# Fetching a second token column by row DMAs from ScalarE, with output rows and layer blocks a step later, in a recommender forward pass

## The chip, the cores and the metric

The kernel runs on one core of one Trainium2 chip. The metric is device time in microseconds (us). A median of three runs without a profiler is the time that counts; one more execution was recorded by the hardware profiler, and everything that is read line by line comes from it.

## The reference

For each of 16384 rows of the batch:

```python
tok = word_emb[token_idx].mean(axis=1)            # 32 tokens, table 50000 x 300, f32
e1, e2, e3 = emb_mh1[mh1_idx].mean(axis=1), ...   # 20 lookups each, tables 1000/5000/10000 x 64
o1, o2, o3, o4 = emb_oh1[oh1_idx], ...            # one lookup each, tables 100/50/20/1000 x 64
emb = concatenate([tok, e1, e2, e3, o1, o2, o3, o4])          # 748 columns
wide = sum over the same small lookups of their wide_* weights  # one number per row
h = relu(emb @ W1 + b1); h = relu(h @ W2 + b2); h = relu(h @ W3 + b3)   # 1024, 512, 256
out = sigmoid(h @ Wd + bd + wide)
```

The token means need 16384 x 32 rows of 1200 bytes from device memory. The small tables are held on the chip and looked up by multiplication with counts.

## The kernel before

**Tiles and steps.** The batch is cut into 128 tiles of 128 rows. A tile has 11 steps (`STEPS`), and 27 more steps (`WAKE`) close the run: 1435 steps in one Python loop that writes out the order of the instructions of every engine by hand. A step has, in order: the next one-hots, the counts, part of the small sums, columns and rows of fetched tokens, tokens, part of the layers, the evictions that are due.

**Tokens.** `tokens()` walks 16 pairs of tokens per tile. For each token GpSimd issues an indirect DMA (line 303) that gathers 128 rows, one per partition, into a pair buffer `tok_rows` (6 buffers). Three pairs later `add_up` adds the two on VectorE (lines 279, 281, 286) into a sum in PSUM; the last addition of a tile writes its features `g`.

**Fetched tokens.** For tiles from 4 on whose number is not a multiple of three (83 tiles) the last token, number 31, isn't gathered by GpSimd. `load_column` (line 320) loads that column of indices into one partition, on SP's queue; `column_offsets` (lines 329, 330) turns them into byte offsets on VectorE. Then `fetch` loads 32 offsets at a time into SP's registers (line 338) and issues 128 DMAs of one row each on SP (line 347), spread over `FETCH_STEPS` = 16.5 steps. It starts 25 or 19.5 steps before the tile's sum is due (`FETCH_AHEAD`). The tile of rows is `fetched`, with two buffers.

**Small lookups.** VectorE compares keys with an iota to make one-hots `hot` (line 402), ScalarE scales their upper half (line 409), TensorE multiplies pairs of one-hots into counts `pc` (line 420), ScalarE evicts these to `cnt` (line 423). The one-hots are made a step before they are counted. A tile later TensorE multiplies the counts with the tables (`terms`, line 455) and VectorE reduces the sums into `g` (line 445).

**Layers.** A finished tile's features are transposed (line 496) and evicted to `x` with a scale (line 500). Tiles are put together in blocks of three (32 blocks), near the end of two (12) and one (8). A block's layers are a generator: `layer` issues f32 matmuls into one of two PSUM buffers `ph` (line 573) and leaves the eviction to ScalarE (line 584) pending until the last matmul of the next group. The driving loop asks the generator for as much work as the step's share. After the third layer `mlp` multiplies with the column `Wd` into `po` (line 605). `finish`, which is queued in `rows_out` and flushed a step later, adds `wide` on VectorE (line 612), takes the sigmoid on ScalarE (line 613) and leaves the store to SP (line 617) two steps on. A block's layers start in the same step in which its last transposes have been issued, after a `flush` of their evictions.

The part of the loop that drives the fetches:

```python
for at, t_f in fetches:
    if step == int(at) - COLUMN_AHEAD:
        load_column(t_f)
    if step == int(at) - COLUMN_LAG:
        column_offsets(t_f)
    if step == int(at):
        fetching.append((at, Paced(fetch(t_f))))
for at, rows in list(fetching):
    rows.to(P * (step + 1 - at) / FETCH_STEPS)
```

Of the kernel before, what the change touches and what calls it, by code (L numbers as in the profile page):

```python
# [19 lines left out]
P = 128  # L20
N_TOK, TOK_D = 32, 300
# [9 lines left out]
FETCH_AHEAD = {1: 25.0, 2: 19.5}  # L31
COLUMN_AHEAD = 4
COLUMN_LAG = 1
LOADS = 32
ROW_BYTES = 4 * TOK_D
WAKE = 27
# [41 lines left out]
def kernel(  # L78
# [209 lines left out]
    def tokens():  # L288

        under_way = []  # L290
        for n in range(n_all):
            if n < n_all - TOK_LAG:
                t, q = divmod(n, n_groups)
                it = token_indices[t // NSUB][:, t % NSUB, :].bitcast(U32)
                tok_rows = tokp.tile([P, TOK_GROUP * TOK_D], F32, name="tok_rows")
                rows = []
                for r in range(TOK_GROUP):
                    j = q * TOK_GROUP + r
                    if j == N_TOK - 1 and t in fetched:
# [3 lines left out]
                    nc.gpsimd.indirect_dma_start(  # L303
                        out=rows[-1],
                        out_offset=None,
                        in_=word,
                        in_offset=bass.IndirectOffsetOnAxis(ap=it[:, j : j + 1], axis=0),
                    )
# [5 lines left out]
    fetched, columns = {}, {}  # L314
    word_bytes = word.bitcast(U8).rearrange("n d -> (n d)").unsqueeze(0)

    def load_column(t):
# [6 lines left out]
    def column_offsets(t):  # L324


        column = columns[t]
        low = ROW_BYTES & -ROW_BYTES
        nc.vector.tensor_single_scalar(column, column, ROW_BYTES // low, op=ALU.mult)
        nc.vector.tensor_single_scalar(column, column, low.bit_length() - 1, op=ALU.logical_shift_left)  # L330

    def fetch(t):


        rows = fp.tile([P, TOK_D], F32, name="fetched").bitcast(U8)
        column = columns.pop(t)
        for p0 in range(0, P, LOADS):
            _, values = nc.values_load_multi_w_load_instructions(
                column[:, p0 : p0 + LOADS],
                engines=[mybir.EngineType.SP],  # L340
                min_val=0,
                max_val=(word.shape[0] - 1) * ROW_BYTES,
                skip_runtime_bounds_check_because="the indices are rows of the table",
            )
            for i, value in enumerate(values):
                p = p0 + i
                nc.sync.dma_start(out=rows[p : p + 1, :], in_=word_bytes[:, bass.ds(value, ROW_BYTES)])  # L347
                if p == P - 1:
                    fetched[t] = rows.bitcast(F32)
                yield 1  # L350

    def load_indices(blk):
# [186 lines left out]
    def flush_rows():  # L539
        while rows_out:  # L540
            rows_out.pop(0)()
# [8 lines left out]
    def flush_outputs():  # L550
        while pending:
            pending.pop(0)()
# [5 lines left out]
    def layer(dst, weights, bias, srcs, n_out, part=None):  # L558


        n = N_of(srcs[0])
        for m in range(n_out):
            begun = part is not None and m < len(part)
            ph = part[m] if begun else ps_h.tile([P, N], F32, name="ph", tag="ph")
            for k, src in enumerate(srcs):
                if begun and k < N_EARLY:
                    continue
                if k == len(srcs) - 1:
                    flush_outputs()
# [12 lines left out]

            def evict(m=m, ph=ph):
                nc.scalar.activation(dst[:, m, 0:n], ph[:, 0:n], AF.Relu, bias=bias[:, m : m + 1])  # L584

            pending.append(evict)
            yield 1

    def mlp(block, part=None):


        n = block.n
        flush_rows()
        h1 = hp.tile([P, M1, N], F32, name="h1", tag="odd")
        yield from layer(h1, w1_sb, b1_sb, [block.chunk(k) for k in range(NK)], M1, part)
        h2 = hp.tile([P, M2, N], F32, name="h2", tag="even")
        yield from layer(h2, w2_sb, b2_sb, [h1[:, k, 0:n] for k in range(M1)], M2)
        flush_outputs()
        h3 = hp.tile([P, M3, N], F32, name="h3", tag="odd")
        yield from layer(h3, w3_sb, b3_sb, [h2[:, k, 0:n] for k in range(M2)], M3)  # L600
        po = ps_h.tile([1, N], F32, name="po", tag="ph")
        for k in range(M3):
            if k == M3 - 1:
                flush_outputs()
            nc.tensor.matmul(  # L605
                po[:, 0:n], wd_sb[:, k : k + 1], h3[:, k, 0:n], start=(k == 0), stop=(k == M3 - 1)
            )
            yield 1

        def finish():  # L610
            y = block.wide()
            nc.vector.tensor_add(y, po[:, 0:n].rearrange("o (a b) -> o a b", b=P), y)
            nc.scalar.activation(y, y, AF.Sigmoid, bias=bd_sb)
# [74 lines left out]
    fetches = [(summed_at(t) - FETCH_AHEAD[t % 3], t) for t in range(FETCH_FROM, tiles) if t % 3]  # L688
    fetching = []

    def speed(step):
# [27 lines left out]
    for step in range(n_steps):  # L719
# [30 lines left out]
        if waiting and step >= waiting[0][0]:  # L750
            _, k, ks = waiting[0]
            if k in summed or ks[0] < N_EARLY and k == tiles - 1:
# [9 lines left out]
        for at, t_f in fetches:  # L762
            if step == int(at) - COLUMN_AHEAD:
                load_column(t_f)
            if step == int(at) - COLUMN_LAG:
                column_offsets(t_f)
            if step == int(at):
                fetching.append((at, Paced(fetch(t_f))))
        for at, rows in list(fetching):
            rows.to(P * (step + 1 - at) / FETCH_STEPS)  # L770
            if step + 1 - at >= FETCH_STEPS:
                rows.finish()
                fetching.remove((at, rows))
# [78 lines left out]
```

## Time and profile before

| what | value |
|---|---|
| median of 3 runs | 5056.46 us (5055.42 to 5058.48) |
| the profiled execution | 7254.38 us, its span 7252.4 us |
| granted TensorE clock in the profile | 0.879 |
| busy in the profile: TensorE, VectorE, ScalarE, GpSimd | 5570.4, 3767.8, 2743.5, 3800.6 us |
| gathers by GpSimd (line 303) | 4013, mean 947 ns |
| row DMAs by SP (line 347) | 10624 of 1.2 KB |
| DMA engines, share of the span: software queue, hardware queue | 31.5%, 2.0% |

How to read it: the profiled execution took over 2000 us more than the runs. Busy times and the lengths of single instructions are those of that one execution; shares of the span are shares of its longer time. In the groups of instructions a line gives the source line, the engine, the operation, the tile written and read, the count, busy us and mean ns, and after the bar the idle time of the engine just before these instructions with what ended most of it. "issue" means that the engine waited for nothing the profile shows. In the timeline the columns are start and length in us, and in brackets the idle time before.

### The profile page before, as it was taken

To read this page: it belongs to the slowest core of one execution; us is meant where nothing else is said; L and a number is where in the kernel's file an instruction comes from. 1 tells how busy PE (TensorE), PEld (TensorE's weight loads), DVE (VectorE), ACT (ScalarE), POOL (GpSimd) and SP (SyncE) were. 2 spreads that over 40 slices of the span, in tenths; PEclk is the share of its full clock that TensorE was granted. 3 is DMA by queue.
4 is the path that set the end of the run, shared out by engine and by line. 5 is a ranking of instruction groups with operands and counts; after the bars stand their busy time and mean duration, and the time that the engine had idled before them with its cause. 6 is when DMAs were issued, how large, how long until landed. Compare 5 with 4: busy or idle time off the path is not lost. (4 is left out here: it accounts for less than half of the span.)

```text
span 7252.4 us, 117093 instructions
## 1 busy us (share of the span) xinstructions
PE 5570.4 (77%) x36252; PEld 4062.8 (56%) x36252; DVE 3767.8 (52%) x6830; ACT 2743.5 (38%) x3658; POOL 3800.6 (52%) x4020
## 2 busy tenths in 40 slices
PE   5687777777777777777777777777777777777777
PEld 3455555555555555555555555555555666666676
DVE  4555555555555555555555555555555555555542
ACT  4343333333333333333333333333333433333331
POOL 5555555555555555555555555555555555555543
PEclk8788988888898988898888888889888988888988
DMA  5333333333333333333333333333333333333332
GB/s 154 89 91 89 90 92 90 88 91 90 88 91 89 89 91 88 89 91 90 88 87 92 90 89 89 87 88 92 91 90 87 91 89 86 85 89 90 87 82 63
DMA packets 282526, 653.63 MB, mean 90 GB/s; under 512 B 140443, under 2 KB 151707, under 8 KB 281895
## 3 DMA queue, kind: packets, MB, share of 16 engines
q0 software_dynamic: 192624, 616.65, 31.5%
q1 hardware_dynamic: 89271, 29.49, 2.0%
q8 instruction: 283, 4.64, 0.3%
q14 instruction: 348, 2.85, 0.1%
HBM read 645.64 MB, written 0.07 MB: 89 GB/s over the span
## 5 line engine op out<-in xcount | busy, mean ns | idle before, releaser
L303 POOL DMA_INDIRECT tok_rows<-in_word_emb_dram,it x4013 | 3799.7, 947 | 3405.5 <-DVE own L286 2018.9
L455 PE MATMUL pg<-terms,cnt 128*128 128x195 bf16 x17664 | 2028.9, 264 | 753.1 <-issue 571.2
L455 PEld LDWEIGHTS <-cnt 128*128 128x128 fp8e3 x17664 | 1656.0, 104 | 985.5 <-issue 934.1
L402 DVE TENSOR_TENSOR hot<-own,sc 128x1656 bf16<-128x1656 bf16 (+1 forms) x1408 | 1393.7, 990 | 1440.3 <-remote 1036.4
L423 ACT ACTIVATE cnt<-pc 128x828 uint16<-128x828 f32 (+1 forms) x1408 | 1187.3, 843 | 2083.2 <-remote 1458.4
L573 PE MATMUL ph<-x,w_sb 128*128 128x384 f32 (+5 forms) x4932 | 1674.6, 479 | 212.8 <-issue 83.9
L409 ACT ACTIVATE hot<-hot 64x768 bf16<-64x768 bf16 (+1 forms) x1408 | 1155.3, 820 | 1729.5 <-DVE hot L402 1470.2
L573 PE MATMUL ph<-h,w_sb 128*128 128x384 f32 (+2 forms) x4160 | 1357.2, 467 | 106.1 <-issue 52.5
L573 PEld LDWEIGHTS ph<-x,w_sb 128*128 128x128 f32 (+1 forms) x4932 | 922.0, 211 | 597.6 <-issue 204.2
L420 PEld LDWEIGHTS <-hot 128*128 128x128 bf16 x8192 | 639.8, 104 | 894.2 <-issue 470.8
L420 PE MATMUL pc<-hot 128*128 128x138 bf16 x8192 | 817.7, 236 | 393.9 <-ACT hot L409 211.6
L573 PEld LDWEIGHTS ph<-h,w_sb 128*128 128x128 f32 x4160 | 767.1, 208 | 413.3 <-issue 121.5
L445 DVE TENSOR_REDUCE g<-pg 128x130 f32<-128x390 f32 (+1 forms) x512 | 260.8, 509 | 1352.4 <-remote 566.9
L281 DVE TENSOR_TENSOR own<-own,tok_rows 128x300 f32<-128x300 f32 x1920 | 916.9, 478 | 67.8 <-DMA tok_rows<-in_word_emb_dram,it 5.9
L286 DVE TENSOR_TENSOR own<-own,tok_rows 128x300 f32<-128x300 f32 x1792 | 856.8, 478 | 65.6 <-DMA tok_rows<-in_word_emb_dram,it 3.9
L584 ACT ACTIVATE h<-ph,b_sb 128x384 f32<-128x384 f32 (+2 forms) x723 | 378.9, 525 | 646.5 <-remote 402.1
L500 DVE TENSOR_TENSOR x<-pc,scale 128x768 f32<-128x768 f32 x127 | 121.0, 953 | 218.3 <-PE pc L496 111.4
L389 DVE COPY sc<-pc 128x512 bf16<-128x512 bf16 x64 | 44.2, 690 | 259.6 <-remote 139.8
L605 PE MATMUL po<-h,wd_sb 128*1 128x384 f32 (+2 forms) x208 | 84.3, 494 | 121.6 <-issue 59.9
L496 PE MATMUL pc<-ident,g 128*128 128x128 f32 x762 | 125.5, 307 | 45.7 <-ACT cnt L423 31.0
L496 PEld LDWEIGHTS pc<-ident,g 128*128 128x128 f32 x762 | 97.1, 160 | 59.6 <-ACT cnt L423 39.8
L605 PEld LDWEIGHTS po<-h,wd_sb 128*1 128x1 f32 x208 | 9.0, 81 | 175.6 <-ACT h L584 82.2
(56 smaller groups left out, 497.3 us busy)
## 6 DMA issues: line engine op xcount, KB each, us to landing
fetched<-in_word_emb_dram SPq DMA_DIRECT2D x10624, 1.2 KB
tok_rows<-in_word_emb_dram,it POOLq DMA_INDIRECT x4013
ix<-in_idx_dram SPq DMA_DIRECT2D x64, 64.0 KB
w_sb<-in_W_dram SPq DMA_DIRECT2D x6, 512.0 KB
raw<-in_mh_dram SPq DMA_DIRECT2D x4, 682.5 KB
it<-in_idx_dram SPq DMA_DIRECT2D x64, 32.0 KB
w_sb<-in_W_dram SPq DMA_DIRECT2D x1, 2048.0 KB
column<-in_idx_dram SPq DMA_DIRECT2D x83, 0.5 KB
```

What stands on the lines that cost most here:

```text
L281: nc.vector.tensor_add(tok_sum, tok_sum, a)
L286: nc.vector.tensor_add(to, tok_sum, b)
L303: nc.gpsimd.indirect_dma_start(out=rows[-1], out_offset=None, in_=word, in_offset=bass.IndirectOffsetOnAxis(ap=it[:, j : j + 1], axis=0),)
L402: nc.vector.tensor_tensor(hot[:, 0 : 2 * rows, :].rearrange("p i (n d) -> p i n d", d=2), iota.rearrange("p (n d) -> p n d", d=2).unsqueez ...
L409: nc.scalar.activation(upper, upper, AF.Copy, scale=UPPER)
L420: nc.tensor.matmul(pc[:, k // n, at : at + n_h], hot[:, 2 * k, 0:P], hot[:, 2 * k + 1, :], start=True, stop=True)
L423: nc.scalar.activation(cnt[:, :, b : b + rows].rearrange("l h (g k) -> l h g k", g=2), pc[:, :, 0 : n * n_h].rearrange("l g (k h) -> l h g ...
L445: nc.vector.tensor_reduce(field_columns(features(t), pair), pg[:, 0:n, :].rearrange("p f (c d) -> p f d c", c=3), AX.X, ALU.add,)
L455: nc.tensor.matmul(pg[:, j, :], by_slice[:, h, :], terms[:, h, :], start=(h == h0), stop=(h == h1 - 1))
L496: nc.tensor.transpose(pt[:, j // n, j % n, :], g[:, c : c + P], ident)
L573: nc.tensor.matmul(to, weights[: src.shape[0], k, m * P : (m + 1) * P], src, start=(k == 0), stop=(k == len(srcs) - 1),)
L584: nc.scalar.activation(dst[:, m, 0:n], ph[:, 0:n], AF.Relu, bias=bias[:, m : m + 1])
```

## The change

Three parts.

1. Thirty tiles, 8, 12, ..., 124, have token 30 fetched too, in the same manner but on ScalarE's queue: `load_column` and `column_offsets` as before for its column, then 8 offsets at a time into ScalarE's registers, and 128 row DMAs issued by ScalarE over 38 steps, begun 42 steps before the sum is due. The rows have one buffer of their own. The column of offsets lies in bytes that two constants (`minus_count`, `zeros`), used only while the tables are converted at the start, leave free.
2. The output row. The matmuls with `Wd` move from `mlp` into `finish`; `wide` is added by a one-row matmul into the same PSUM group, so the addition on VectorE goes, and the sigmoid reads PSUM. `finish` is flushed at the latest after the first group of the next block's first layer. The tiles `h1`, `h2`, `h3` are allocated when first written.
3. A block's layers start at the earliest in the step after the one in which its last transposes were issued, and no `flush` stands before them.

```diff
+SCALAR_FROM, SCALAR_EVERY = 8, 4
+SCALAR_STEPS = 38.0
+SCALAR_AHEAD = 42.0
+SCALAR_LOADS = 8
...
+    fa = ctx.enter_context(tc.tile_pool(name="fetched_scalar", bufs=1))
...
-    minus_count = const.tile([P, P], BF16, name="minus_count")
+    early_use = const.tile([P, P // 2 + ROW], I32, name="early_use")
+    minus_count = early_use[:, 0 : P // 2].bitcast(BF16)
...
-    zeros = const.tile([P, ROW], F32, name="zeros")
+    zeros = early_use[:, P // 2 : P // 2 + ROW].bitcast(F32)
...
-                    if j == N_TOK - 1 and t in fetched:
-                        rows.append(fetched.pop(t))
+                    if (t, j) in fetched:
+                        rows.append(fetched.pop((t, j)))
                         continue
...
-        columns[t] = fp.tile([1, P], I32, name="column")
+        columns[t, j] = early_use[0:1, 0:P] if j < N_TOK - 1 else fp.tile([1, P], I32, name="column")
         nc.sync.dma_start(
-            out=columns[t], in_=idx[t * P : (t + 1) * P, N_TOK - 1 : N_TOK].rearrange("n o -> o n")
+            out=columns[t, j], in_=idx[t * P : (t + 1) * P, j : j + 1].rearrange("n o -> o n")
         )
...
-    def fetch(t):
+    def fetch(t, j):
-        rows = fp.tile([P, TOK_D], F32, name="fetched").bitcast(U8)
-        column = columns.pop(t)
-        for p0 in range(0, P, LOADS):
+        by_scalar = j < N_TOK - 1
+        rows = (fa if by_scalar else fp).tile([P, TOK_D], F32, name="fetched").bitcast(U8)
+        column = columns.pop((t, j))
+        queue, engine = (
+            (nc.scalar, mybir.EngineType.Activation) if by_scalar else (nc.sync, mybir.EngineType.SP)
+        )
+        loads = SCALAR_LOADS if by_scalar else LOADS
+        for p0 in range(0, P, loads):
             _, values = nc.values_load_multi_w_load_instructions(
-                column[:, p0 : p0 + LOADS],
-                engines=[mybir.EngineType.SP],
+                column[:, p0 : p0 + loads],
+                engines=[engine],
...
-                nc.sync.dma_start(out=rows[p : p + 1, :], in_=word_bytes[:, bass.ds(value, ROW_BYTES)])
+                queue.dma_start(out=rows[p : p + 1, :], in_=word_bytes[:, bass.ds(value, ROW_BYTES)])
...
         for m in range(n_out):
+            if rows_out:
+                if m:
+                    flush_rows()
+                else:
+                    flush_outputs()
...
-        flush_rows()
-        h1 = hp.tile([P, M1, N], F32, name="h1", tag="odd")
+        h1, h2, h3 = h("h1", M1, "odd"), h("h2", M2, "even"), h("h3", M3, "odd")
...
-        po = ps_h.tile([1, N], F32, name="po", tag="ph")
-        for k in range(M3):
-            if k == M3 - 1:
-                flush_outputs()
-            nc.tensor.matmul(
-                po[:, 0:n], wd_sb[:, k : k + 1], h3[:, k, 0:n], start=(k == 0), stop=(k == M3 - 1)
-            )
-            yield 1
 
         def finish():
+            po = ps_h.tile([1, N], F32, name="po", tag="ph")
+            po = po[:, 0:n].rearrange("o (a b) -> o a b", b=P)
             y = block.wide()
-            nc.vector.tensor_add(y, po[:, 0:n].rearrange("o (a b) -> o a b", b=P), y)
-            nc.scalar.activation(y, y, AF.Sigmoid, bias=bd_sb)
+            nc.tensor.matmul(po, ident[0:1, 0:1], y, start=True, stop=False)
+            for k in range(M3):
+                nc.tensor.matmul(
+                    po,
+                    wd_sb[:, k : k + 1],
+                    h3()[:, k, 0:n].rearrange("p (a b) -> p a b", b=P),
+                    start=False,
+                    stop=(k == M3 - 1),
+                )
+            nc.scalar.activation(y, po, AF.Sigmoid, bias=bd_sb)
...
-    mlp_work = NK * M1 + M1 * M2 + M2 * M3 + M3
+    mlp_work = NK * M1 + M1 * M2 + M2 * M3
...
+    fetches += [
+        (summed_at(t) - SCALAR_AHEAD, SCALAR_STEPS, t, N_TOK - 2)
+        for t in range(SCALAR_FROM, tiles, SCALAR_EVERY)
+    ]
...
                 if not block.missing:
                     complete.append(block)
-        if complete and layers is None:
-            flush(step)
-            block = complete.pop(0)
-            layers, target = start(block), 0
+                    completed = step
+        if complete and layers is None and step > completed:
+            layers, target = start(complete.pop(0)), 0
...
     Paced(mlp(block, part)).finish()
+    flush_outputs()
     flush_rows()
```

More of the change, by code (lines that the diff above doesn't have):

```diff
@@ L315, with load_column, column_offsets @@
     word_bytes = word.bitcast(U8).rearrange("n d -> (n d)").unsqueeze(0)
-    def load_column(t):
-        columns[t] = fp.tile([1, P], I32, name="column")
+    def load_column(t, j):
+        columns[t, j] = early_use[0:1, 0:P] if j < N_TOK - 1 else fp.tile([1, P], I32, name="column")
         nc.sync.dma_start(
-            out=columns[t], in_=idx[t * P : (t + 1) * P, N_TOK - 1 : N_TOK].rearrange("n o -> o n")
+            out=columns[t, j], in_=idx[t * P : (t + 1) * P, j : j + 1].rearrange("n o -> o n")
         )
-    def column_offsets(t):
-        column = columns[t]
+    def column_offsets(t, j):
+        column = columns[t, j]
         low = ROW_BYTES & -ROW_BYTES
@@ L346, in fetch @@
                 p = p0 + i
-                nc.sync.dma_start(out=rows[p : p + 1, :], in_=word_bytes[:, bass.ds(value, ROW_BYTES)])
+                queue.dma_start(out=rows[p : p + 1, :], in_=word_bytes[:, bass.ds(value, ROW_BYTES)])
                 if p == P - 1:
-                    fetched[t] = rows.bitcast(F32)
+                    fetched[t, j] = rows.bitcast(F32)
                 yield 1
@@ L583, in evict @@
             def evict(m=m, ph=ph):
-                nc.scalar.activation(dst[:, m, 0:n], ph[:, 0:n], AF.Relu, bias=bias[:, m : m + 1])
+                nc.scalar.activation(dst()[:, m, 0:n], ph[:, 0:n], AF.Relu, bias=bias[:, m : m + 1])
             pending.append(evict)
@@ L592, in mlp, with h, get @@
         n = block.n
-        flush_rows()
-        h1 = hp.tile([P, M1, N], F32, name="h1", tag="odd")
+        hidden = {}
+        def h(name, m, tag):
+            def get():
+                if name not in hidden:
+                    hidden[name] = hp.tile([P, m, N], F32, name=name, tag=tag)
+                return hidden[name]
+            return get
+        h1, h2, h3 = h("h1", M1, "odd"), h("h2", M2, "even"), h("h3", M3, "odd")
         yield from layer(h1, w1_sb, b1_sb, [block.chunk(k) for k in range(NK)], M1, part)
-        h2 = hp.tile([P, M2, N], F32, name="h2", tag="even")
-        yield from layer(h2, w2_sb, b2_sb, [h1[:, k, 0:n] for k in range(M1)], M2)
+        yield from layer(h2, w2_sb, b2_sb, [h1()[:, k, 0:n] for k in range(M1)], M2)
         flush_outputs()
-        h3 = hp.tile([P, M3, N], F32, name="h3", tag="odd")
-        yield from layer(h3, w3_sb, b3_sb, [h2[:, k, 0:n] for k in range(M2)], M3)
-        po = ps_h.tile([1, N], F32, name="po", tag="ph")
-        for k in range(M3):
-            if k == M3 - 1:
-                flush_outputs()
-            nc.tensor.matmul(
-                po[:, 0:n], wd_sb[:, k : k + 1], h3[:, k, 0:n], start=(k == 0), stop=(k == M3 - 1)
-            )
-            yield 1
+        yield from layer(h3, w3_sb, b3_sb, [h2()[:, k, 0:n] for k in range(M2)], M3)
         def finish():
+            po = ps_h.tile([1, N], F32, name="po", tag="ph")
+            po = po[:, 0:n].rearrange("o (a b) -> o a b", b=P)
             y = block.wide()
-            nc.vector.tensor_add(y, po[:, 0:n].rearrange("o (a b) -> o a b", b=P), y)
-            nc.scalar.activation(y, y, AF.Sigmoid, bias=bd_sb)
+            nc.tensor.matmul(po, ident[0:1, 0:1], y, start=True, stop=False)
[8 more added lines that the diff above has]
+            nc.scalar.activation(y, po, AF.Sigmoid, bias=bd_sb)
             b0 = block.first * P
@@ L686, in summed_at @@
         return n / FRONT_PACE if n < front else FRONT_STEPS + (n - front) / pace
-    fetches = [(summed_at(t) - FETCH_AHEAD[t % 3], t) for t in range(FETCH_FROM, tiles) if t % 3]
+    fetches = [
+        (summed_at(t) - FETCH_AHEAD[t % 3], FETCH_STEPS, t, N_TOK - 1)
+        for t in range(FETCH_FROM, tiles)
+        if t % 3
+    ]
+    fetches += [
+        (summed_at(t) - SCALAR_AHEAD, SCALAR_STEPS, t, N_TOK - 2)
+        for t in range(SCALAR_FROM, tiles, SCALAR_EVERY)
+    ]
     fetching = []
@@ L757 @@
                     complete.append(block)
-        if complete and layers is None:
-            flush(step)
-            block = complete.pop(0)
-            layers, target = start(block), 0
-        for at, t_f in fetches:
+                    completed = step
+        if complete and layers is None and step > completed:
+            layers, target = start(complete.pop(0)), 0
+        for at, n, *of in fetches:
             if step == int(at) - COLUMN_AHEAD:
-                load_column(t_f)
+                load_column(*of)
             if step == int(at) - COLUMN_LAG:
-                column_offsets(t_f)
+                column_offsets(*of)
             if step == int(at):
[L768 to L771, printed above, removed]
+                fetching.append((at, n, Paced(fetch(*of))))
+        for entry in list(fetching):
+            at, n, rows = entry
+            rows.to(P * (step + 1 - at) / n)
+            if step + 1 - at >= n:
                 rows.finish()
-                fetching.remove((at, rows))
+                fetching.remove(entry)
         toks.to(tokens_by(step + 1))
```

## The prediction

> **What bounds the kernel now.** I read the page's engine totals first, then the groups of instructions, then GpSimd's timeline, and last the waits.
>
> ```profile
> PE 5570.4 (77%) x36252; PEld 4062.8 (56%) x36252; DVE 3767.8 (52%) x6830; ACT 2743.5 (38%) x3658; POOL 3800.6 (52%) x4020
> ...
> L303 POOL DMA_INDIRECT tok_rows<-in_word_emb_dram,it x4013 | 3799.7, 947 | 3405.5 <-DVE own L286 2018.9
> ```
>
> By shares TensorE (PE) looks like the limit at 77%, and GpSimd (POOL) idles 3405 us. But this execution took 7254.38 us and the median of the runs is 5056.46 us, so the profile shows 2198 us that the runs don't have. The shares can't be read as they stand; I look for what the extra time is and which engine's work fills 5056 us.
>
> GpSimd's timeline from 3013 us, and SP's beside it:
>
> ```profile
> 3013.99 0.95 POOL L303 DMA_INDIRECT tok_rows<-in_word_emb_dram,it  x1 [0.30 <-issue]
> 3015.24 0.95 POOL L303 DMA_INDIRECT tok_rows<-in_word_emb_dram,it  x1 [0.30 <-issue]
> 3016.49 0.95 POOL L303 DMA_INDIRECT tok_rows<-in_word_emb_dram,it  x1 [0.30 <-issue]
> 3017.74 0.94 POOL L303 DMA_INDIRECT tok_rows<-in_word_emb_dram,it  x1 [0.30 <-issue]
> 3018.99 0.95 POOL L303 DMA_INDIRECT tok_rows<-in_word_emb_dram,it  x1 [0.31 <-issue]
> ```
> ```profile
> 3010.14 5.75 SPq L347 DMA_DIRECT2D fetched<-in_word_emb_dram  x19
> ```
>
> A gather starts 1.25 us after the one before: 0.947 busy and 0.30 in which it waits for nothing shown. This period is the commonest of all (median of the 4012 start-to-start times 1.250 us). Now 4012 × 1.2505 = 5017 us, against 5056.5 in the runs; what is left, 39.5 us, must hold the head and the tail. The first gather starts at 2.96 us, the last one here:
>
> ```profile
> 7205.74 0.95 POOL L303 DMA_INDIRECT tok_rows<-in_word_emb_dram,it  x1 [0.30 <-DVE own L286]
> ...
> 7249.77 0.40 ACT L613 ACTIVATE x<-x,bd_sb 1x128 f32<-1x128 f32 x1 [0.78 <-DVE x L612]
> ```
>
> So head and tail were 3 and 46.6 us, the tail with a halt of TensorE of some 8 us. They already fill the remainder. In an undisturbed run the gathers run back to back: **GpSimd is the bound**, its idle time an effect of this profile. The extra 2198 us fits stretches in which SP's row issues and TensorE's matmuls come 0.70 us apart for 3 to 7 us at a time (3006.6 to 3010.2, 3015.9 to 3021.3) while the gathers keep their 1.25 us; outside them SP issues a row each 0.3 us (5.75 us for 19 above; the commonest step is 0.323). Summed over SP's and TensorE's records I estimate such stretches at 2650 to 2900 us, enough for the difference. Then GpSimd waits for rows to be added (its waits, longest first):
>
> ```profile
> POOL tok_rows L303 <- DVE own L286: 2018.9, 602, 12.7
> ```
>
> **How near the others are.** In undisturbed stretches a 384-wide f32 matmul record takes 0.325 us (4 in 1.46 us less the drain), a 195-wide bf16 one 0.086, a 138-wide one 0.060. Times their counts (5632 records of 384, 2112 of 256 at 0.218, 1408 of 128 at 0.112: 2448 us; L455 1519; L420 492; the rest some 250) TensorE needs about 4710 us: 93% of 5056, the second bound. VectorE needs 3768 us plus gaps, some 80%. A row on SP costs 0.323 us (29 ns move, 228 ns issue, gaps) and each 32 offsets a register load of 2.04 us, so a fetched token takes SP 128 × 0.323 + 4 × 2.2 = 50.2 us, and 83 of them 4167 us (82%). ScalarE (ACT) is busy 2743 us (54%), 1.91 us per step over 1435 steps of 3.52 us.
>
> **What the Trainium skill says.** "Advanced Engine Details and Errata" (Sequencer Loop, Engine Queue Depths): an engine instruction is pushed into a queue, 8 deep on ScalarE, where it waits for its semaphores, while the sequencer goes on to control instructions. That would let DMA issues run beside activations; ScalarE issues none in this trace. "Perfetto Trace Analysis" (DMA Instruction — HWDGE) has one descriptor generator behind a lock, shared by its sequencers; the trace shows SP alone, 228 ns each. "DMA: Bandwidth & Descriptors" (Issuing engines are not separate DMA queues) says that a second issuing engine saves only issue time; that is what is sought here, and the DMA engines are 31.5% + 2% busy. Its section Latency and other measured facts gives a register load a floor of some 600 ns; 2.04 us for 32 registers is the nearest row.
>
> **The change, part by part.**
>
> 1. *Gathers removed.* Tiles 8, 12, ..., 124, 30 of them, lose the gather of token 30. 30 × 1.2505 = **37.5 us off the binding engine**. GpSimd's queue has nothing else. The gathers that follow start one period sooner; the 6 pair buffers (12 gathers, 15 us) let GpSimd run that far ahead of VectorE's additions.
>
> 2. *Rows on ScalarE.* 30 × 128 = 3840 row issues, each with its move, and 30 × 16 loads of 8 offsets. At SP's 0.323 us a row and 0.6 us a load (2.04/4 = 0.51 from below, 2.04 from above) a token is 41.3 + 9.6 = 50.9 us, 1528 us in all, spread over 38 steps: 1.34 us on each of 1140 steps. Behind a burst (3.4 rows and 0.4 of a load) stand the layer evictions and the next step's scaling of the one-hots; TensorE waits for both. Even one after the other, 1.91 + 1.34 = 3.25 us is below the new step of 3.50. The one-hots are scaled a step before they are counted and a layer has a second PSUM buffer, so I count it at 0, with 0.25 us per step as the cover. Bounds: -0 (no reason for a gain) and, if it all stands on the path, the second rival's price.
>
> 3. *Rows' landing.* Issue ends 4 steps, 14 us, before the sum; VectorE's wait for the fetched rows was 0.6 us in all with SP's 3-step margin. 0. The single buffer is free 3 steps before the next fetch.
>
> 4. *Columns.* SP gets 30 more loads of 0.41 us and some gap, about 20 us (4167 to 4190, hidden in 5020); VectorE 60 more scalings, 30 × (239 + 226) ns = 14 us.
>
> 5. *Output row.* VectorE loses 52 additions (L612: 17.1 + 4.9 + 2.2 = 24 us). TensorE gains 52 matmuls of one row, two records each: 64 × 0.325 + 24 × 0.218 + 16 × 0.112 = 28 us (42 by the mean of L605's row). It loses the wait for the last eviction ahead of L605, 142 us here in 57 waits, most in halts; I take 1 us × 52. TensorE ends at 4690 to 4740 of 5020. On the path: 0. The sigmoid then reads PSUM, and SP's store waits for it as before, with rows queued behind it on SP.
>
> 6. *Layers a step later.* TensorE no longer meets a block whose x is just being evicted (69 us by L500 here); hidden, 0. At the end a step's layer work (about 2 us) may slip behind the last gather, and the last row loses a hop to VectorE (0.5 us). I add 1 us; bounds -1 to +3.
>
> **Sum.** On the median: head 3 + 3982 × 1.2505 + tail 36.5 = 5019, and 1 = **5020 us**, -0.7%. The profiled execution (7254) is not bound by gathers and gets about 8200 more records; it will rather be longer, and I sum against the runs only. An effect under 0.2% (10 us) can't be told from none here.
>
> **Rivals.**
>
> *TensorE takes over at once (0.07).* If the gather in an undisturbed run takes less than 1.25 us, TensorE with 4710 us and its unseen dependences bounds the run, 28 us more and about 50 us of waits less. For: 93% is near. Against: 4012 periods fill the time to within 10 us. Time: 5056 - 22 = 5034 to 5066. That the change takes no gathers away is excluded by the code: `fetched` is looked up by (tile, token).
>
> *ScalarE's in-order issue (0.16), slower.* Place: the rows between the eviction of counts (L423) and the next scaling (L409). If the sequencer handles a row only when the activations ahead are done, each of 1140 steps costs 1.91 + 1.34 and the two gaps of clean steps (0.23 and 0.25), 3.73 us instead of 3.50: +262 us, 5282. It decides from 0.25 us exposed per step; 0.33 gives 5020 + 1140 × 0.08 = 5111. For: ScalarE stands on the chain one-hot, scaling, count. Against: ScalarE waited 1470 us for VectorE's one-hots, time in which rows can go out.
>
> *SP starved by the shared generator (0.07), slower.* Three tiles give SP 2 × 50.2 + 4 us of 117.3 now. From 50 ns more per row it is late, and VectorE stops at L286. At 70 ns: 20 ns × 256 × 41 = +210 us. A lock held 0.2 us for 3.4 rows in 3.5 us meets SP a fifth of the time: 20 ns on average, below the point.
>
> **Numbers.** The first case has 0.70: 5003 to 5050, the low end if the 10 us by which head, tail and gathers overfill the runs come off the tail and some 7 us of small stalls go too, the high end if 30 us of ScalarE's bursts show. With 0.07 for TensorE's case and some 0.08 of the slower cases' 0.23 the range runs to 5111, rounded to 5110, and leaves about 0.15 out. Faster by over 0.2% (below 5046): 0.68 of the first case and 0.02 of TensorE's, 0.70. Within 0.2%: the rest of these two and 0.01 of the slower ones, 0.08. Slower: 0.22.
>
> **What would show it.** L303 with 3983 gathers, still 1.25 us apart where not held; new row issues on ScalarE's queue near 228 ns; L409 and L423 no later after VectorE and TensorE than now; SP's row at 323 ns still; no wait of VectorE for fetched rows; L612 gone. The forecast is wrong if rows on ScalarE take much over 0.33 us, or activations wait behind them, or SP's rows slow by over 50 ns.

## The result, and the profile after

The changed kernel takes 5947.38 us (median of five runs, 5942.94 to 5951.95); the kernel before beside it 5056.46 us (5055.42 to 5058.54). The ratio is 1.1759 (95% interval 1.1746 to 1.1773): 891 us slower, where 5020 us was forecast. The profiled execution of the changed kernel has a span of 5940.9 us, so its profile can be read as its runs. The profiled execution of before (7254 us), and one group of experiments below in which before took 7368 us without a profiler, belong to a rarer kind of execution in which the whole program takes over 40% longer; no conclusion below rests on them.

The page of the changed kernel: engine totals, then the groups of the gathers, of the column offsets and of the last addition of a tile with rows from SP. After the bar stands the idle time of the engine just before these instructions, and what ended most of it.

```profile
PE 4988.0 (84%) x36356; PEld 3850.3 (65%) x36356; DVE 3756.7 (63%) x6838; ACT 2735.6 (46%) x3658; POOL 3770.0 (63%) x3990
...
L309 POOL DMA_INDIRECT tok_rows<-in_word_emb_dram,it x3983 | 3769.1, 946 | 2143.2 <-DVE own L292 921.9
...
L335 DVE TENSOR_SCALAR column<-column 1x128 int32<-1x128 int32 x83 | 17.9, 215 | 995.1 <-DMA column<-in_idx_dram 987.7
...
L292 DVE TENSOR_TENSOR g<-own,fetched 128x300 f32<-128x300 f32 x83 | 39.1, 471 | 179.9 <-DMA fetched<-in_word_emb_dram 178.4
```

The gathers are as short as ever (946 ns) and there are 30 fewer, but GpSimd now waits 922 us for additions on VectorE, and VectorE has a new stop of 988 us: at line 335, where it waits for a column of indices to arrive. In the profile of before the same two groups of VectorE hardly wait (lines 329 and 286 there), and in experiment 1 below, an execution of the usual length, they wait as little (0.0 and 0.3 us):

```profile
L286 DVE TENSOR_TENSOR g<-own,fetched 128x300 f32<-128x300 f32 x83 | 39.0, 470 | 3.4 <-DMA fetched<-in_word_emb_dram 0.6
...
L329 DVE TENSOR_SCALAR column<-column 1x128 int32<-1x128 int32 x83 | 19.8, 239 | 0.3 <-issue 0.3
```

Columns are loaded by SP. The new row DMAs on ScalarE look harmless in themselves. So the question is why SP is late.

SP's own waits in the changed kernel (engine, line, what it waited for: us in total, times, longest):

```profile
SPq L358 <- DMA fetched<-in_word_emb_dram: 1280.6, 1424, 14.6
```

SP's row DMAs (line 358) wait 1281 us for *earlier row DMAs*. A smaller wait of this kind was in the profile of before, and the prediction did not look at it:

```profile
SPq L347 <- DMA fetched<-in_word_emb_dram: 157.8, 351, 1.6
```

That execution took 7254 us; in experiment 1, of the usual length and with SP's rows alone, such waits add up to 37 us by the single records.

The single records give the reason. Each DMA of SP and of ScalarE signals its completion on one of eight semaphores, numbered 101 to 108, and the two engines share the eight. Of the row DMAs of the changed kernel none starts sooner than 1.21 us after the one before it on its semaphore, and the ones that had to wait start some 1.9 us after it. The trace also has the signals of landing: of the 2014 rows of both engines that start over 0.15 us after the instruction before them, three quarters start 15 to 20 ns after the last such signal on their own semaphore. So a DMA goes out when the previous one on its semaphore has landed. I added up the time SP stands before a row by whose DMA was last on that semaphore: **1177 us in 1172 waits behind a row of ScalarE**, 197 us behind its own.

The timeline shows one such hold. The columns are start and length in us, engine, line, operation; in brackets the idle time before.

```profile
3005.48 10.99 SPq L358 DMA_DIRECT2D fetched<-in_word_emb_dram  x16
...
3007.52 0.21 DVE L335 TENSOR_SCALAR early_use<-early_use 1x128 int32<-1x128 int32 x1 [3.55 <-DMA early_use<-in_idx_dram]
...
3011.33 0.84 ACT L420 ACTIVATE hot<-hot 64x768 bf16<-64x768 bf16 x1 [4.18 <-DVE hot L413]
...
3012.48 1.39 ACTq L358 DMA_DIRECT2D fetched<-in_word_emb_dram  x4
```

SP needs 11 us for 16 rows here. By its single records it issues a row at 3010.70, wants to issue the next at about 3010.96 on semaphore 101, and can only at 3014.46. The DMA before it on 101 is the first row of ScalarE, issued at 3012.48, whose last signal of landing comes at 3014.44; that row stands behind a load of offsets, which starts at 3011.34, with the activation of line 420 (3011.33) that had waited 4.18 us for VectorE's one-hots; and VectorE had itself stood 3.55 us waiting for a column from SP. The waits close a circle: SP, ScalarE, VectorE, SP.

What that does to SP as a whole, from its records (first row of one token to first row of the next, mean over 82 intervals):

| kernel | a token, first to last row | pause to the next token | period |
|---|---|---|---|
| parts 2 and 3 of the change alone | 51.1 us | 7.8 us | 58.9 us |
| the changed kernel | 66.8 us | 2.8 us | 69.9 us |

The first column holds all that SP does between the two rows: loads of offsets, of columns and of indices. A load of 32 offsets takes 2.1 us, so a pause of 2.8 us is no pause: SP's queue hardly rests. 82 x (69.9 - 58.5) = 935 us, with 58.5 the period of the version with separate semaphores below; that version's span is 917 us shorter. So the lengthening of SP's period is as large as the whole loss; that SP is the cause and not carried along by a kernel that is slow for another reason, experiments 3 to 5 have to show.

### The profile page after: what moved, and what is told of

Its sections match the earlier page's. It is cut to its first block, busy times and chain, and to the rows that moved or that the text cites. A ratio compares the mean times of both kernels' runs of the same rounds, so it can differ in the third digit from the quotient of the medians.

```text
span 5940.9 us, 125681 instructions
## 1 busy us (share of the span) xinstructions
PE 4988.0 (84%) x36356; PEld 3850.3 (65%) x36356; DVE 3756.7 (63%) x6838; ACT 2735.6 (46%) x3658; POOL 3770.0 (63%) x3990
## 4 chain that ended last, share of the span: by engine, by line
PE 57%; SPq 13%; DMA 11%; DVE 9%; issue 6%; ACT 2%; POOL 1%; ACTq 1%; DVEq 0%; POOLq 0%
PE ph L589 29%; PE pg L466 19%; SPq L358 10%; PE pc L431 6%; DMA fetched<-in_word_emb_dram 5%; DVE hot L413 3%; DMA column<-in_idx_dram 3%; SPq L349 3%; DVE own L287 2%; DVE own L292 2%; DMA tok_rows<-in_word_emb_dram,it 2%; ACT hot L420 1%; POOL tok_rows L309 1%; PE pc L507 1%; PE po L631 1%
## 5 line engine op out<-in xcount | busy, mean ns | idle before, releaser
L466 PE MATMUL pg<-terms,cnt 128*128 128x195 bf16 x17664 | 1804.2, 256 | 212.4 <-DVE g L456 212.4
L466 PEld LDWEIGHTS <-cnt 128*128 128x128 fp8e3 x17664 | 1592.5, 101 | 217.3 <-issue 176.2
L589 PE MATMUL ph<-x,w_sb 128*128 128x384 f32 (+5 forms) x4932 | 1517.8, 447 | 50.1 <-ACT h L600 35.7
L431 PEld LDWEIGHTS <-hot 128*128 128x128 bf16 x8192 | 610.2, 100 | 1092.1 <-ACT hot L420 718.0
L589 PE MATMUL ph<-h,w_sb 128*128 128x384 f32 (+2 forms) x4160 | 1263.0, 444 | 34.9 <-ACT h L600 34.9
L431 PE MATMUL pc<-hot 128*128 128x138 bf16 x8192 | 759.1, 230 | 613.3 <-ACT hot L420 575.5
L589 PEld LDWEIGHTS ph<-x,w_sb 128*128 128x128 f32 (+1 forms) x4932 | 856.7, 196 | 356.1 <-ACT h L600 41.2
L589 PEld LDWEIGHTS ph<-h,w_sb 128*128 128x128 f32 x4160 | 722.0, 196 | 300.1 <-ACT h L600 42.5
L292 DVE TENSOR_TENSOR g<-own,fetched 128x300 f32<-128x300 f32 x83 | 39.1, 471 | 179.9 <-DMA fetched<-in_word_emb_dram 178.4
```

Source lines behind the costliest of these rows:

```text
L292: nc.vector.tensor_add(to, tok_sum, b)
L431: nc.tensor.matmul(pc[:, k // n, at : at + n_h], hot[:, 2 * k, 0:P], hot[:, 2 * k + 1, :], start=True, stop=True)
L466: nc.tensor.matmul(pg[:, j, :], by_slice[:, h, :], terms[:, h, :], start=(h == h0), stop=(h == h1 - 1))
L589: nc.tensor.matmul(to, weights[: src.shape[0], k, m * P : (m + 1) * P], src, start=(k == 0), stop=(k == len(srcs) - 1),)
```

## The experiments

In all of them "bound by gathers" means head, tail and 1.2505 us a gather: n x 1.2505 + 39.5 us for n gathers, which is within 1 us the sum of the prediction.

**1. Parts 2 and 3 of the change alone** (output rows and blocks a step later, no token for ScalarE).

```diff
-        for t in range(SCALAR_FROM, tiles, SCALAR_EVERY)
+        for t in range(SCALAR_FROM, 0, SCALAR_EVERY)
```

> The changed kernel without ScalarE's rows: only the output row by TensorE and the layers a step later are left, gathers stay 4013. Theory (SP and ScalarE share eight completion semaphores for their row DMAs, and a row is issued only when the last row on its semaphore has landed, so SP waits for rows that ScalarE has not yet issued): no rows on ScalarE, so 5056 within 10 us. Rival A (ScalarE's rows delay its own activations): the same, 5056. Rival B (the new order of layers and output rows costs the time): about 5900.

5055.11 us against 5057.27, ratio 0.9995 (0.9986 to 1.0004). These parts cost and bring nothing. Its profiled span is 5054.4 us, and its gathers start 1.2511 us apart on average over the whole run: the reading that gathers run back to back in undisturbed runs was right.

**2. Part 1 alone** (ScalarE's rows, with the layers and output rows of before).

```diff
...
-        h1, h2, h3 = h("h1", M1, "odd"), h("h2", M2, "even"), h("h3", M3, "odd")
+        flush_rows()
+        h1 = hp.tile([P, M1, N], F32, name="h1", tag="odd")
...
-        if complete and layers is None and step > completed:
-            layers, target = start(complete.pop(0)), 0
+        if complete and layers is None:
+            flush(step)
+            block = complete.pop(0)
+            layers, target = start(block), 0
...
```

> The kernel before with ScalarE's rows alone; output rows and layers as before. Theory and rival A: about 5950, within 60 us of the changed kernel. Rival B (the new order is at fault): 5019, the forecast for the removed gathers.

5998.16 us, ratio 1.1855 (1.1836 to 1.1875). All of the loss is in ScalarE's rows; beside them the other parts even seem worth some 50 us (5998 against 5947, from two groups of runs).

**3. ScalarE's rows without SP's** (token 31 is gathered by GpSimd in every tile).

```diff
-        for t in range(FETCH_FROM, tiles)
+        for t in range(FETCH_FROM, 0)
```

> The changed kernel with SP's fetches of token 31 given back to GpSimd: 4066 gathers, ScalarE's 3840 rows are the only rows left. Theory: nobody on SP to be held up, the gathers bind, 4065 x 1.2505 + 39.5 = 5123, up to 5160. Rival A: ScalarE issues as many rows between as many activations as in the changed kernel, so the 0.8 us per step stay: 5900 or more.

5122.13 us (5120.03 to 5122.65); bound by 4066 gathers it would be 5124. So 3840 row DMAs and 480 loads of offsets on ScalarE cost the kernel nothing by themselves. ScalarE's issue of rows between its activations is not the cause.

**4. Separate semaphores.** All of the change, with the same rows at the same places, but ScalarE's rows signal on four semaphores of their own (99 to 102 in the trace, while SP's DMAs use eight others, 105 to 112), and VectorE waits for these before the one addition that needs the rows.

```diff
...
-            nc.vector.tensor_add(tok_sum, tok_sum, a)
...
+                nc.vector.wait_ge(own_sems[nth // 8], 16 * P * (nth % 8 + 1))
+            ins = nc.vector.tensor_add(tok_sum, tok_sum, a)
...
+                    ins.then_inc(own_sems[(t - SCALAR_FROM) // SCALAR_EVERY // 8], 16)
+                    tc.no_tile_sem_insts.add(ins.ins.name)
...
```

> The changed kernel, but ScalarE's rows count on semaphores of their own (one for eight tokens, VectorE waits for the sum of all 128 rows before it adds), so that no row of SP waits for one of ScalarE or the other way round; the same rows, loads and gathers. Theory: 5020 to 5060. Rival A (ScalarE's time): 5900. Rival C (the descriptor generator shared by SP and ScalarE slows both): 5900, with SP's rows well over 0.323 us apart.

5025.18 us (5023.22 to 5026.6), ratio 0.9936 (0.9919 to 0.9953): faster than before, and 5 us from the forecast. The engine totals and the gathers of its page:

```profile
PE 4810.4 (96%) x36356; PEld 3725.4 (74%) x36356; DVE 3735.3 (74%) x6838; ACT 2727.8 (54%) x3658; POOL 3770.9 (75%) x3990
...
L316 POOL DMA_INDIRECT tok_rows<-in_word_emb_dram,it x3983 | 3770.0, 947 | 1219.3 <-issue 732.8
```

The idle time before gathers is 1219 us, as in a kernel bound by them, with "issue" as its largest part; in the changed kernel it was 2143. SP's waits for fetched rows are no longer among its longest; by the records they add up to 37 us. The rows, their loads and their places are those of the changed kernel; what differs is the semaphores and the waits that went with sharing them. So **the shared semaphores are the cause**.

Two limits of this experiment. It takes away the waits in both directions, and those of ScalarE's rows for earlier rows of their own, for its rows here wait for nothing. In the changed kernel ScalarE too is held behind rows of SP: some 125 us before its own rows, and 288 us of idle time before the activations of line 420 end when a row has landed. That SP's full queue is what makes the sharing costly, experiment 5 shows; how the 927 us divide between the two directions was not measured. And the granted clock of TensorE fell with the loss, to 0.915 in the changed kernel from 0.989 here. A slower TensorE alone doesn't explain the loss: it is busy 4988 us there and 4810 here, 178 us more, while its standing time grows from 213 to 953 us. Whether some of the 178 us is in the 927 stays open.

**5. SP with half its tokens** (42 in place of 83), semaphores shared.

```diff
-        if t % 3
+        if t % 3 == 1
```

> The changed kernel, semaphores shared as in it, but SyncE fetches the last token of 42 tiles (those with t % 3 = 1) instead of 83; ScalarE's 30 tokens stay. 4096 - 72 = 4024 gathers are left on GpSimd. Theory (SyncE's queue, held up by ScalarE's rows on the semaphores the two share, is late because it was nearly full already): the half-empty queue has room for the waits, and GpSimd's gathers bind again at 4024 x 1.2505 + 39.5 = 5071 us (5060 to 5110), although 41 more gathers are left than in the changed kernel. Rival (ScalarE's rows hold up the kernel directly, or each wait of SyncE costs the kernel its length whatever the load): between 5450 and 5950 us.

5072.13 us (5066.76 to 5073.47), within about a microsecond of the theory's 5071. Its waits and its page:

```profile
SPq L358 <- DMA fetched<-in_word_emb_dram: 899.3, 848, 13.1
```
```profile
L309 POOL DMA_INDIRECT tok_rows<-in_word_emb_dram,it x4024 | 3807.6, 946 | 1229.9 <-issue 734.0
```

SP still waits 899 us for rows, and it costs nothing: between two of its tokens it now rests 45 us. Here the waits of SP cost time only when its queue is full.

**6. ScalarE for every eighth tile** (15 tokens), semaphores shared.

```diff
-SCALAR_FROM, SCALAR_EVERY = 8, 4
+SCALAR_FROM, SCALAR_EVERY = 8, 8
```

> The changed kernel with ScalarE fetching for every eighth tile (15 tokens), at the same pace while it does. 3998 gathers are left, which would bind at 3998 x 1.2505 + 39.5 = 5039 us. Theory: SyncE loses about 39 us of waiting per ScalarE token (1177 us over 30), and has about 18% of 8 x 39.5 us = 57 us to spare in eight tiles, so it catches up between two such tokens, but the lead of a fetch (8.5 steps, some 33 us) is a little shorter than the loss: 5100 us (5040 to 5250), that is much less than half of the 922 us that the changed kernel exceeds its 5025. Rival (the cost goes with the number of ScalarE's rows, whatever SyncE has to spare): half of it, 5039 + 461 = 5500 us.

5413.95 us (5408.47 to 5417.02): a miss, near the rival. SP's period shows why: 63.3 us, with 3.0 us between tokens, so SP does not rest in any part of this run. I had taken 18% of SP's time as spare, from a sum of row issues and loads; with everything that its queue does, a token takes about 51.1 + 2.8 = 53.9 us of 58.9, which leaves 5.0 us, 8%, or some 410 us in all. SP waited 718 us behind ScalarE and the kernel lost 375 over its gathers.

**7. Separate semaphores, every third tile** (40 tokens).

```diff
-SCALAR_FROM, SCALAR_EVERY = 8, 4
-SCALAR_STEPS = 38.0
-SCALAR_AHEAD = 42.0
+SCALAR_FROM, SCALAR_EVERY = 8, 3
+SCALAR_STEPS = 27.0
+SCALAR_AHEAD = 30.0
...
```

> The version in which ScalarE's rows have semaphores of their own, with a fetch for every third tile (40 tokens in place of 30, each spread over 27 steps in place of 38 and begun 30 steps ahead in place of 42). 3973 gathers are left. Theory (gathers bind): 10 x 1.2505 = 12.5 us below the 5025 of the version with every fourth tile, 5013 us (5008 to 5018). Rival (TensorE, at 4830 us of work in some 5025, or ScalarE's queue, which now issues 4.7 rows a step, takes over as the bound): 5025 us or more.

5016.3 us (5015.7 to 5018.55), ratio 0.9919 (0.9905 to 0.9933), the fastest of all. It gains 9 us of the 12.5. In its trace the gathers lose 12.9 us over a strict 1.2505 us each, in experiment 4 7.4 and in experiment 3 0.8: something else begins to show. TensorE, 96% busy, is a likely candidate; that was not tested.

**8. The same 15 tokens, spread over twice as many steps.** Here my idea of *how* the shared semaphores cost time was put to the test: eight transfers in flight, too few for two engines when ScalarE issues four rows at once.

```diff
-SCALAR_FROM, SCALAR_EVERY = 8, 4
-SCALAR_STEPS = 38.0
-SCALAR_AHEAD = 42.0
+SCALAR_FROM, SCALAR_EVERY = 12, 8
+SCALAR_STEPS = 76.0
+SCALAR_AHEAD = 80.0
```

> As with every eighth tile (15 tokens of ScalarE, 1920 rows, shared semaphores), but each token is spread over 76 steps in place of 38 and begun 80 ahead in place of 42, so that ScalarE issues one or two rows at a time in place of three or four; first tile 12. 3998 gathers are left, 5039 us if they bind. Theory (SyncE and ScalarE together have eight transfers in flight, each some 1.9 us from issue to landing: at SyncE's 0.32 us a row its turn of eight takes 2.56 us and has room for two rows of ScalarE, not for four): SyncE's waits behind ScalarE's rows fall from 718 us to below 350, and the time to 5039 to 5110 us. Rival (each row of ScalarE costs SyncE the same 0.37 us whenever it comes, as for a ScalarE that issues late behind a waiting activation): 718 us again and 5414 us.

6170.26 us (6165.74 to 6177.64): neither. Half as many rows as in the changed kernel cost more than all of them, and SP waited 1552 us behind ScalarE. Too few places in flight for bursts of four rows is refuted, and so is a fixed price per row. The timeline:

```profile
2976.03 19.54 SPq L358 DMA_DIRECT2D fetched<-in_word_emb_dram  x34
2976.15 0.53 ACTq L358 DMA_DIRECT2D fetched<-in_word_emb_dram  x2
2980.19 0.21 ACTq L358 DMA_DIRECT2D fetched<-in_word_emb_dram  x1
2983.59 0.53 ACTq L358 DMA_DIRECT2D fetched<-in_word_emb_dram  x2
2986.35 0.53 ACTq L358 DMA_DIRECT2D fetched<-in_word_emb_dram  x2
2995.67 0.54 SPq L326 DMA_DIRECT2D column<-in_idx_dram  x1
...
2997.85 0.21 DVE L335 TENSOR_SCALAR column<-column 1x128 int32<-1x128 int32 x1 [13.26 <-DMA column<-in_idx_dram]
```

ScalarE issues a row or two per step, at 2980.2, 2983.6 and 2986.4. In SP's single records a row follows 1.3 to 1.75 us after each of these, on the same semaphores 107, 108 and 102, and almost nothing goes out between: SP may not run ahead of ScalarE, and in this stretch is held once per step. From 2987.7 it is free and issues 25 rows at 0.32 us, but by then VectorE has been standing at line 335 for 3 us, with the column load behind those 25 rows.

**9 and 10. No usable time.** These two kernels, repeated as 11 and 12, belong to the group in which before took 7368 us: 7542.69 us, ratio 1.0235 (1.0206 to 1.0263), and 8242.15 us, ratio 1.1195 (1.1174 to 1.1217).

> Every eighth tile (15 tokens of ScalarE, 1920 rows, shared semaphores) as before, each token now spread over 27 steps in place of 38 (31 steps ahead in place of 42): 405 steps with rows of ScalarE in place of 570; in the slow version they were 1140. 3998 gathers are left, 5039 us if they bind. Theory (SyncE is held once in each step in which ScalarE issues rows, however many, until the row that comes before it on its semaphore has landed, since it may not run ahead of ScalarE; measured 718 us in 570 steps and 1552 us in 1140, 1.3 us a step): 405 x 1.3 = 530 us of waits, some 340 us of it absorbed as in the two others (718 - 375, 1552 - 1131), 5039 + 190 = 5230 us (5150 to 5300). Rival 1 (each row costs the same): 5414 us. Rival 2 (eight transfers in flight at once are too few, so that denser rows cost more): over 5450 us.

> The changed kernel, but SyncE loads the columns of its own fetches eight steps ahead in place of four. 3983 gathers are left, 5020 us if they bind. Theory (SyncE's queue is full: 69.9 us from the start of one token to the next against 58.5 needed, with only the register load between two tokens): VectorE's wait at the column falls from 988 us to below 300, and the time goes into its wait for the fetched rows (178 us now) instead; 5850 to 5960 us. Rival (VectorE stops only because the column stands behind a few steps of rows in SyncE's queue, and stops ScalarE, which then holds SyncE up in turn): the earlier column breaks the circle, 5050 to 5400 us.

**11. The same 15 tokens in fewer steps.**

```diff
-SCALAR_FROM, SCALAR_EVERY = 8, 4
-SCALAR_STEPS = 38.0
-SCALAR_AHEAD = 42.0
+SCALAR_FROM, SCALAR_EVERY = 8, 8
+SCALAR_STEPS = 27.0
+SCALAR_AHEAD = 31.0
```

> The kernel with 15 tokens of ScalarE over 27 steps each once more, since the kernel before took 7368 us beside it the first time, in place of 5057. As then: theory (a hold of 1.3 us in each step in which ScalarE issues rows) 5230 us (5150 to 5300); rival 1 (each row costs the same) 5414 us; rival 2 (eight transfers in flight are too few) over 5450 us.

5139.47 us (5131.44 to 5151.79). Both rivals are far off; the theory has the direction and overstates the size, for the time lies below its 5150. The four kernels together:

| kernel | tokens of ScalarE | steps with its rows | SP's wait behind ScalarE | time over the gathers |
|---|---|---|---|---|
| 11 | 15 | 405 | 376 us | 100 us |
| 6 | 15 | 570 | 718 us | 375 us |
| the change | 30 | 1140 | 1177 us | 927 us |
| 8 | 15 | 1140 | 1552 us | 1131 us |

SP's wait goes with the number of steps in which ScalarE issues rows, 0.9 to 1.4 us each, rather than with the number of rows, 0.20 to 0.81 us each. The wait exceeds the loss by 250 to 420 us in the four kernels, which is the order of SP's spare time, about 410 us.

**12. SP's columns loaded eight steps ahead**, in place of four.

```diff
-            if step == int(at) - COLUMN_AHEAD:
+            if step == int(at) - (COLUMN_AHEAD + 4 * (n == FETCH_STEPS)):
```

> The kernel with the columns of SyncE loaded eight steps ahead once more, for the same reason. As then: theory (SyncE's queue is full, the wait only moves from the column to the fetched rows) 5850 to 5960 us; rival (the column's place behind rows in SyncE's queue closes a circle of waits, which an earlier column breaks) 5050 to 5400 us.

5870.52 us (5867.78 to 5873.9), as the theory had it. The stop only moves, from the column to the rows:

```profile
L292 DVE TENSOR_TENSOR g<-own,fetched 128x300 f32<-128x300 f32 x83 | 39.0, 470 | 636.3 <-DMA fetched<-in_word_emb_dram 632.3
...
L335 DVE TENSOR_SCALAR column<-column 1x128 int32<-1x128 int32 x83 | 19.2, 231 | 238.8 <-DMA column<-in_idx_dram 238.8
```

SP's period is 69.0 us against 69.9. The column is where lateness shows first, not where it comes from. ScalarE's own columns, through which the circle of the timeline above ran, were not moved; VectorE waits for them 48 us in all in the changed kernel and 194 us here.

## Why the prediction was wrong

**Reading of the bound: right.** Gathers back to back at 1.25 us bind the undisturbed run. Experiments 3, 5, 1 and 4, with 4066, 4024, 4013 and 3983 gathers, came to 5122.1, 5072.1, 5055.1 and 5025.2 us; worked out: 5124.0, 5071.5, 5057.8 and 5020.2. TensorE, the second bound, was put somewhat too low: 4710 us, where it is busy 4832 us (96%) in experiment 1.

**Part 1, the gathers removed: right.** 37.5 us forecast. With the obstacle gone, experiment 4 is 32 us faster than before.

**Part 2, rows on ScalarE: the step that failed.** It asked what the new instructions cost ScalarE and who waits for ScalarE's activations. What they do to SP's queue, which issues the same kind of DMA, it put at nothing; only a rival with a chance of 0.07 asked, and only for the descriptor generator. "I count it at 0, with 0.25 us per step as the cover" holds for ScalarE (experiment 3); the missing term is the wait at the shared semaphores: SP stands 1177 us for ScalarE's rows, and the kernel ends 927 us over its gathers. The sizes were fair: a row takes 0.311 to 0.317 us in a burst (0.323 taken), most loads of eight offsets 0.72 to 0.86 us (0.6 taken), and neither matters.

**Part 3, landing: wrong by the same term.** VectorE's wait for fetched rows, put at 0, became 178 us, on rows of SP that were late.

**Part 4, SP: the reserve mis-sized.** The 20 us of more column loads did no harm, as experiment 4 shows, but SP's spare time was taken from a sum of rows and loads (50.2 us a token, 82%). Measured over its whole period it is 53.9 of 58.9 us, 92%.

**Parts 5 and 6: right in that they are hidden.** Experiment 1 shows no effect, -0.05% with an interval of 0.09% on either side. One reading in part 5 counts twice: the 142 us ahead of line 605 add up 60 us of waits of the matmuls and 82 us of their weight loads, which overlap. Nothing rests on it.

**The rivals.** TensorE did not take over. That ScalarE's in-order issue costs time, the rival given most chance, is refuted by experiments 3 and 4. "SP starved by the shared generator" named the place and the victim: SP late, VectorE stopped. Its sign, SP's rows slower by over 50 ns, came true too: 1177 us over 10624 rows are 0.11 us a row. But its mechanism was another one. Its price came from 20 ns more per issue; SP's issue takes 228 ns in the changed kernel, 228 in experiment 1 and 229 in experiment 4, so the shared generator that the Trainium skill describes ("Perfetto Trace Analysis", DMA Instruction — HWDGE) does not slow SP's issue here. The wait stands before the issue, for a semaphore. Hence 210 us where it was 927, and a range that ended at 5110.

**Two expectations from pages.** In the Trainium skill, "DMA: Bandwidth & Descriptors" (Issuing engines are not separate DMA queues) says that a second issuing engine saves issue time alone. Experiment 4 agrees in that there is a saving, 32 us. The changed kernel shows that it can also cost, when both engines' DMAs signal on the same semaphores. "Advanced Engine Details and Errata" (Sequencer Loop, Engine Queue Depths) made me expect that ScalarE's sequencer would get to control instructions while an activation waits. The timeline above disagrees: the load of offsets starts at 3011.34, 0.01 us after an activation that had stood 4.18 us. It is no single case: in the changed kernel 49 loads of offsets, and 206 of the register moves that precede a row, start within 0.03 us after the start of an activation that had waited over 1 us. Only a small part of the loss is that lateness, though: of SP's 1177 us, 182 pass before the ScalarE row in question has been issued and 995 while it is on its way.

**Open.** The order in which the two queues' DMAs take turns on the eight semaphores was not varied by itself; why a step with ScalarE's rows costs 0.9 us in one kernel and 1.4 in another is therefore not explained.

## What to carry to other kernels

Before a second engine gets DMAs to issue, look in the trace on which semaphores the DMAs of both complete, and give the new queue its own: a queue that shared them could not run ahead of the other, and here that decided between -0.6% and +17.6%. It cost nothing where the first queue was half empty (experiment 5). Where they must be shared, few steps with many rows cost less here than many steps with few. And take a queue's reserve from its measured period and pauses in a run, not from a sum over its instructions: 82% by the sum was 92% in fact.

## What the hardware showed that I had not expected

- A queue stands before a DMA until the previous DMA on the same completion semaphore has landed; held rows start 15 to 20 ns after that signal. With SP alone on eight semaphores this cost 37 us in all (experiment 1, single records), with ScalarE's rows on them SP's waits for rows became 1281 us.
- Spreading the same 1920 rows over 76 steps a token, in place of 27, raised the time from 5139 to 6170 us. With shared semaphores, spreading is not gentler.
- Row DMAs from two engines at once cost each other next to nothing at the issue. On SP an issue takes 228 ns on average with ScalarE's rows and without; on ScalarE 247 ns with SP's rows and 245 without (experiment 3), mostly 213, with some 450 for the first row after a load.
